# Two transformer layers on one core: where the causal mask of 384- and 512-key diagonal blocks is added in the row maximum of layer 0

## The chip, the core and the metric

The kernel runs on one core of a Trainium2 chip. Five engines work side by side, each through its own queue in order: TensorE (PE in the profile, PEld for its weight loads), VectorE (DVE), ScalarE (ACT), GpSimd (POOL), and SyncE (SP), which here issues DMAs only. They tell each other of finished work through semaphores. The metric is the device time of one execution in microseconds (us); a kernel's time is the median of its runs.

## The reference, cut to what matters

Two transformer layers act on x of shape 2 x 1024 x 256. Each adds an attention and a feed-forward branch to x. The change touches the attention of layer 0 only: 32 query heads of 8 numbers, 8 key heads (four query heads share one), 1024 positions, with a causal mask:

```python
xn = _layernorm(x)
q = (xn @ Wq + bq)...; k = (xn @ Wk + bk)...; v = (xn @ Wv + bv)...   # 32, 8, 8 heads of 8
q = q * cos + rotate_half(q) * sin;  k = k * cos + rotate_half(k) * sin
scores = einsum('bhqd,bhkd->bhqk', q, k_rep) / sqrt(8)
scores = where(kpos > qpos, -inf, scores)
attn = softmax(scores);  out = einsum('bhqk,bhkd->bhqd', attn, v_rep)
x = x + out @ Wo + bo + ffn0(xn)
```

The softmax subtracts each row's maximum over the keys up to the row's own position. Layer 1 has another attention without a causal mask and its own feed-forward branch; it follows after layer 0.

## The kernel before, in words

Layer 0 takes queries in 16 tiles of 128 rows, written (b, i): batch b is 0 or 1, i from 0 to 7. The order is (0,0) to (0,7), then (1,7) down to (1,0). Each tile is handled twice.

**First pass, the maximum** (`max_unit`). For one head pair (16 pairs `p`; the two heads of a pair lie in the upper and the lower 64 rows of the TensorE array, index `e`), TensorE multiplies queries by keys (line 1012) into two PSUM tiles of 512 columns, one for each e, and VectorE takes the negated maximum of each with one `tensor_reduce` from PSUM (line 1024) into a column of the tile `mx`. Tiles with i > 3 first have 16 units over 512 keys that need no mask (`part` 1). Then come the units of the diagonal block (`part` 0, `masked`). Their width is 128, 256, 384 or 512 keys for i mod 4 = 0, 1, 2 or 3, and a unit holds n = 4, 2, 1 or 1 head pairs. The mask is added by TensorE: `add_mask` (line 984) multiplies an identity matrix (`ident_h`) by a triangle of -1e30 (`mask_q`) into the last 128 columns, with four products and four weight loads for one head pair (two halves t, two heads e), 128 and 64 columns wide. The maximum can start when the last of them is done.

**Second pass, the weights** (`weigh`, `gather`). TensorE forms the scores again, transposed and with the maximum folded in as additional rows (line 1076); ScalarE takes the exponential (line 1086); GpSimd zeroes what is above the diagonal (line 1090); TensorE multiplies by the values (line 1106).

PSUM tiles of the first pass come from the pool `ps_s` with three buffers (tag "s"). A unit needs two, so the second product of a unit waits until a maximum of the unit ahead has been read; TensorE's order is written out by hand (`manual_schedule`), so all that stands behind that product waits too. The function `one_slot` sets that order: a credit in columns (`cost`) decides how many units of the first pass go ahead of each piece of the second pass, and pieces of layer 0's feed-forward branch (`ffn0`, lines 216 to 318 on VectorE) and other preparations are dealt out between them. The order of the other engines comes from a scheduler, in queues that run strictly in order.

Constants (`ident_h`, `mask_q`, both made by GpSimd at the start) lie in the pool `zp`, which is freed after layer 0; scratch tiles of layer 0's attention come from `pool`.

Of the kernel before, what the change touches and what calls it, by code (L numbers as in the profile page):

```python
# [10 lines left out]
F32 = mybir.dt.float32  # L11
BF = mybir.dt.bfloat16
# [4 lines left out]
ALU = mybir.AluOpType  # L17
# [3 lines left out]
P = 128  # L21
# [16 lines left out]
NEG = -1e30  # L38
# [11 lines left out]
def two_layers(ctx: ExitStack, tc: tile.TileContext, a: dict, out: bass.AP):  # L50
    nc = tc.nc
    cp = ctx.enter_context(tc.tile_pool(name="const", bufs=1))
    layer0 = ExitStack()
    zp = layer0.enter_context(tc.tile_pool(name="layer0", bufs=1))
# [20 lines left out]
    for name, op, fill, sign in (  # L75
# [5 lines left out]
        for e in range(2):  # L81
            for t in range(2):
                part = m[HALF * e : HALF * e + HALF, t, :]
                nc.gpsimd.affine_select(
                    out=part,
                    in_=part,
                    compare_op=op,
                    fill=fill,
                    base=sign * HALF * t,
                    pattern=[[-sign, P]],  # L90
                    channel_multiplier=sign,
                )
    ident_h, mask_q = both.values()
    groups = cp.tile([P, P], BF, tag="groups", name="groups")
    nc.vector.memset(groups, 0.0)
    nc.vector.memset(groups[0:64, 0:64], 1.0)
# [695 lines left out]
    def attention0(w, qlast, tables):  # L792
# [10 lines left out]
        scale = 1.0 / HD0**0.5  # L803
        with ExitStack() as es:
            pool = es.enter_context(tc.tile_pool(name="a0", bufs=2))
# [170 lines left out]
            def add_mask(out, start, stop):  # L976


                for t in range(2):
                    lo = HALF * t  # L980
                    for e in range(2):
                        rows = slice(HALF * e, HALF * e + HALF)
                        rhs = mask_q[rows, t, None, lo:]
                        nc.tensor.matmul(  # L984
                            out[e][:, :, lo:],
                            ident_h[rows, t, :],
                            rhs.to_broadcast([HALF, out[e].shape[1], P - lo]),
                            start=start and t == 0,
                            stop=stop and t == 1,
                        )  # L990
# [6 lines left out]
            mx = {}  # L997
            reduced = None

            def max_unit(b, i, pairs, lo, width, part, masked):  # L1000
                if (b, i) not in mx:
                    mx[b, i] = pool.tile([P, 2, 2, NH0 // 2], F32, tag="mx", name=f"mx{b}{i}", bufs=3)
                n = len(pairs)
                assert (b, lo // 512) in loaded
                sc = [ps_s.tile([P, 512], F32, tag="s", name=f"m{b}{i}_{pairs[0]}_{part}{e}") for e in range(2)]
                four = masked and width == P
                if four:
                    add_mask([x.rearrange("p (h k) -> p h k", h=4) for x in sc], True, False)
                for s, p in enumerate(pairs):
                    for e in range(2):  # L1010
                        rows = slice(HALF * e, HALF * e + HALF)
                        nc.tensor.matmul(  # L1012
                            sc[e][:, s * width : (s + 1) * width],
                            qst[b, i][0][rows, p, :],
                            kst[b][0][rows, lo // 512, p // 4, 0:width],
                            start=not four,
                            stop=s == n - 1 if four else not masked,
                        )
                    if masked and not four:
                        end = (s + 1) * width  # L1020
                        add_mask([x[:, None, end - P : end] for x in sc], False, True)
                nonlocal reduced
                for e in range(2):
                    reduced = nc.vector.tensor_reduce(  # L1024
                        mx[b, i][:, part, e, pairs[0] : pairs[0] + n],
                        sc[e][:, : n * width].rearrange("p (s k) -> p s k", s=n),
                        AX.X,
                        ALU.max,
                        negate=True,
                    )  # L1030
# [27 lines left out]
            def max_units(b, i):  # L1058

                if i > 3:  # L1060
                    for p in range(16):
                        yield 1024, lambda p=p: max_unit(b, i, [p], 0, 512, 1, False)
                lo = 512 * (i // 4)
                width = (i % 4 + 1) * P
                n = (4, 2, 1, 1)[i % 4]
                for p in range(0, 16, n):
                    yield 2 * n * width, lambda p=p: max_unit(b, i, list(range(p, p + n)), lo, width, 0, True)
                yield 0, lambda: take_max(b, i)
# [375 lines left out]
```

## Time and profile before

| | |
|---|---|
| median of three runs | 1149.86 us (1149.62 to 1157.1) |
| profiled execution, own time | 1152.2 us |
| its span, first to last instruction | 1150.4 us |
| mean granted TensorE clock | 0.927 |
| PE / DVE / ACT / POOL busy, share of the span | 88% / 66% / 53% / 35% |
| line 1024, maxima on VectorE | 608 instructions, 373.0 us busy |
| line 984, mask products on TensorE | 832 products, 73.7 us busy |

Busy time of TensorE overlaps with itself, since products are pipelined and the two halves of the array run side by side: 73.7 us of mask products are not 73.7 us of time. What a line is worth is told by the chain of waits, which follows the work that ended last back from the end. All of the first pass lies between 45 us and 734 us of the span; layer 1 fills the rest.

### The profile page before, as it was taken

What the parts mean: (1) busy time and instruction counts of PE and PEld (TensorE: products, weight loads), DVE (VectorE), ACT (ScalarE), POOL (GpSimd) and SP (SyncE); (2) the same over time, 40 slices, a digit from 0 to 9 for tenths busy, and PEclk for the clock granted to TensorE, in tenths of its full rate; (3) what the DMA queues carried; (4) which work ended last, traced back from release to release, by engine and by line L of the source; (5) the groups of instructions that cost most, each with busy time, mean ns of one, the idle gap of its engine ahead of it and who ended that gap; (6) DMA issues with size and microseconds to landing.
All of it is one profiled execution on the core that took longest, in us unless ns stands there. A gap on an engine that the chain in (4) does not pass through costs nothing.

```text
span 1150.4 us, 19967 instructions
## 1 busy us (share of the span) xinstructions
PE 1008.0 (88%) x7676; PEld 483.0 (42%) x7699; DVE 761.3 (66%) x1434; ACT 607.9 (53%) x1097; POOL 400.4 (35%) x440
## 2 busy tenths in 40 slices
PE   5858797897998989998989989987999999898897
PEld 2333332232432313232323333334567677576576
DVE  6567977889687898889796879413554544543531
ACT  3014571674455757688867766852564444433431
POOL 2007224324135121412123254554744535413400
PEclk9758896998899989999999999998899999989998
DMA  5432101101102010100010110008522332331100
GB/s 176 120 103 75 53 2 40 21 21 41 55 3 51 6 28 10 37 10 8 21 24 5 28 26 6 5 7 103 86 49 47 79 58 43 82 63 34 39 20 20
DMA packets 65927, 49.04 MB, mean 43 GB/s; under 512 B 20904, under 2 KB 59432, under 8 KB 65832
## 3 DMA queue, kind: packets, MB, share of 16 engines
q1 hardware_dynamic: 60632, 39.05, 15.0%
q0 software_dynamic: 4112, 8.26, 3.0%
q8 instruction: 60, 0.98, 0.4%
q10 hardware_dynamic: 1088, 0.46, 0.1%
q14 instruction: 35, 0.29, 0.1%
HBM read 34.12 MB, written 15.20 MB: 43 GB/s over the span
## 4 chain that ended last, share of the span: by engine, by line
PE 53%; DVE 25%; DMA 8%; ACT 6%; POOL 3%; issue 3%; SPq 2%; DVEq 0%; ACTq 0%; POOLq 0%
DVE mx L1024 13%; PE acc L1106 8%; PE s L1076 7%; PE f1gu L672 5%; PE sk L551 4%; PE f1o L711 3%; PE m L1012 3%; PE pqk L465 3%; PE sq L516 3%; DMA qscr<-ptq 2%; PE gu L301 2%; ACT p L1086 2%; DMA qs<-mscr 2%; SPq L936 2%; DMA qkv<-all 2%
## 5 line engine op out<-in xcount | busy, mean ns | idle before, releaser
L1024 DVE TENSOR_REDUCE mx<-m 128x1 f32<-128x512 f32 (+3 forms) x608 | 373.0, 653 | 99.8 <-PE m L1012 53.3
L1086 ACT ACTIVATE p<-s 128x512 f32<-128x512 f32 x576 | 307.6, 606 | 123.1 <-PE s L1076 119.1
L1106 PE MATMUL acc<-p,v 128*9 128x512 f32 x1152 | 170.4, 610 | 1.8 <-ACT p L1086 1.2
L1090 POOL TENSOR_SCALAR_AFFINE_SELECT p<-p 128x512 f32<-128x512 f32 x128 | 83.0, 673 | 152.6 <-ACT p L1086 152.4
L1012 PE MATMUL m<-k,qmain 64*128 64x512 bf16 (+3 forms) x384 | 95.1, 357 | 43.7 <-DVE mx L1024 34.4
L1012 PE MATMUL m<-kmain,qmain 64*128 64x512 bf16 (+3 forms) x384 | 81.7, 330 | 21.8 <-DVE mx L1024 19.9
L1012 PEld LDWEIGHTS <-qmain 64*128 64x128 bf16 x768 | 50.3, 98 | 80.9 <-issue 52.0
L984 PEld LDWEIGHTS <-ident_h 64*128 64x128 bf16 x832 | 45.7, 97 | 82.7 <-issue 59.8
L984 PE MATMUL m<-mask_q,ident_h 64*128 64x128 bf16 (+3 forms) x832 | 73.7, 221 | 1.8 <-DVE mx L1024 1.7
L1076 PE MATMUL s<-qmain,k 64*128 64x512 bf16 x288 | 65.7, 394 | 6.3 <-DVE att L1129 2.7
L1076 PE MATMUL s<-qmain,kmain 64*128 64x512 bf16 x288 | 65.3, 385 | 6.7 <-ACT p L1086 4.2
L1076 PE MATMUL s<-qlast,k 35*128 35x512 bf16 x288 | 62.8, 390 | 0.0
L1076 PE MATMUL s<-qlast,klast 35*128 35x512 bf16 x288 | 61.5, 381 | 0.0
L1076 PEld LDWEIGHTS <-k 64*128 64x128 bf16 (+1 forms) x576 | 21.0, 95 | 93.0 <-issue 84.5
L672 PEld LDWEIGHTS <-wgu_bf 128*128 128x128 bf16 x384 | 38.5, 101 | 42.4 <-issue 6.8
L681 DVE SCALAR_TENSOR_TENSOR h<-h,f1gu 128x512 f32<-128x512 f32 x32 | 22.0, 686 | 51.6 <-ACT h L680 51.6
L686 POOL TENSOR_TENSOR sq<-h 128x512 f32<-128x512 f32 x28 | 29.1, 1040 | 70.3 <-DVE h L682 67.5
L551 PE MATMUL sk<-qs,ks 25*128 25x128 f32 x512 | 45.3, 424 | 7.7 <-DMA qs<-mscr 7.6
L1149 POOL TENSOR_TENSOR x<-x,aos 128x256 f32<-128x256 f32 x16 | 12.6, 788 | 112.6 <-ACT aos L1148 112.6
L559 ACT ACTIVATE p<-sk 128x2048 f32<-128x2048 f32 x16 | 30.0, 1878 | 41.0 <-PE sk L551 41.0
L524 DVE TENSOR_REDUCE m<-sq 128x16 f32<-128x2048 f32 x16 | 36.6, 2287 | 21.8 <-PE sq L516 21.7
L154 POOL TENSOR_TENSOR hp<-hrest,hp 128x512 bf16<-128x512 f32 x32 | 37.0, 1157 | 34.8 <-ACT hp L153 34.8
(288 smaller groups left out, 1803.1 us busy)
## 6 DMA issues: line engine op xcount, KB each, us to landing
qmain<-qscr SPq DMA_DIRECT2D x64, 96.0 KB
qkv<-all SPq DMA_DIRECT2D x16, 384.0 KB
qscr<-ptq POOLq DMA_DIRECT2D x6, 384.0 KB, 4.2
x<-in_x SPq DMA_DIRECT2D x16, 128.0 KB
qmain<-qscr SPq DMA_DIRECT2D x32, 64.0 KB
qs<-qkv SPq DMA_DIRECT2D x16, 128.0 KB
ks<-qkv SPq DMA_DIRECT2D x16, 128.0 KB
vs<-qkv SPq DMA_DIRECT2D x16, 128.0 KB
```

What stands on the lines that cost most here:

```text
L154: engines[1].tensor_tensor(parts[2], r, parts[1], ALU.subtract)
L465: nc.tensor.matmul(pqk, x[k], wqk[:, k, :], start=(k == 0), stop=(k == 1))
L524: last(nc.vector.tensor_reduce(m, ps, AX.X, ALU.max, negate=True))
L551: nc.tensor.matmul(ps[:, s, r, :], columns(k, slice(S * s, S * s + HD + 9), 4 * b + r), columns(q, slice(S * s, S * s + HD + 9), 4 * b + r ...
L672: nc.tensor.matmul(ps[g], wgu_bf[:, k, g * HID + hc * P : g * HID + (hc + 1) * P], x_parts[n][m][:, k, :], start=(k == 0 and m == 0), stop ...
L984: nc.tensor.matmul(out[e][:, :, lo:], ident_h[rows, t, :], rhs.to_broadcast([HALF, out[e].shape[1], P - lo]), start=start and t == 0, stop ...
L1012: nc.tensor.matmul(sc[e][:, s * width : (s + 1) * width], qst[b, i][0][rows, p, :], kst[b][0][rows, lo // 512, p // 4, 0:width], start=not ...
L1024: reduced = nc.vector.tensor_reduce(mx[b, i][:, part, e, pairs[0] : pairs[0] + n], sc[e][:, : n * width].rearrange("p (s k) -> p s k", s=n ...
L1076: nc.tensor.matmul(sc[e], kst[b][n][rows, j // 4, u, j % 4 * P : (j % 4 + 1) * P], qst[b, i][n][rows, 4 * u : 4 * u + 4, :], start=n == 0, ...
L1086: nc.scalar.activation(p, sc[e], AF.Exp, scale=scale)
L1090: nc.gpsimd.affine_select(out=by_head, in_=by_head, compare_op=ALU.is_ge, fill=0.0, base=0, pattern=[[0, 4], [1, P]], channel_multiplier=-1,)
L1106: nc.tensor.matmul(acc[32 * s : 32 * s + HD0 + 1, :], vst[b][:, j, 4 * G + s, :], ps[s], start=(j == 0), stop=(j == i),)
```

## The change

For units of one head pair (n = 1, that is i mod 4 = 2 with 384 keys and i mod 4 = 3 with 512 keys) the four mask products are left out. VectorE takes the maximum with `tensor_tensor_reduce` in the place of `tensor_reduce`: it adds the scores in PSUM to a tile of float32 in SBUF (`later_keys`, -1e30 after the diagonal and 0 elsewhere, its last 384 or 512 columns), multiplies by -1 and takes the minimum into the column of `mx`. The instruction also writes its elementwise result, to a bfloat16 tile `unused` with one buffer that nobody reads. Units with n = 4 and n = 2 keep their mask products, and units without a mask keep `tensor_reduce`. GpSimd makes `later_keys` at the start with two instructions. The area of SBUF that holds descriptors of DMAs issued by GpSimd is set to 4096 bytes of a partition.

```diff
     ident_h, mask_q = both.values()
+    later_keys = zp.tile([P, 512], F32, tag="later_keys", name="later_keys")
+    nc.gpsimd.memset(later_keys, 0.0)
+    nc.gpsimd.affine_select(out=later_keys, in_=later_keys, compare_op=ALU.is_ge, fill=NEG,
+        base=512 - P, pattern=[[-1, 512]], channel_multiplier=1)
...
-                            stop=s == n - 1 if four else not masked,
-                        )
-                    if masked and not four:
+                            stop=s == n - 1 if four else not masked or n == 1,
+                        )
+                    if masked and not four and n > 1:
                         end = (s + 1) * width
                         add_mask([x[:, None, end - P : end] for x in sc], False, True)
                 for e in range(2):
+                    if masked and n == 1:
+                        unused = pool.tile([P, 512], BF, tag="unused", name=f"unused{b}{i}{pairs[0]}{e}", bufs=1)
+                        reduced = nc.vector.tensor_tensor_reduce(
+                            out=unused[:, 0:width],
+                            in0=sc[e][:, 0:width],
+                            in1=later_keys[:, 512 - width : 512],
+                            scale=-1.0,
+                            scalar=-NEG,
+                            op0=ALU.add,
+                            op1=ALU.min,
+                            accum_out=mx[b, i][:, part, e, pairs[0] : pairs[0] + 1],
+                        )
+                        continue
                     reduced = nc.vector.tensor_reduce(
...
-    nc = _bacc.Bacc("TRN2", target_bir_lowering=False, num_devices=1)
+    nc = _bacc.Bacc("TRN2", target_bir_lowering=False, num_devices=1, dynamic_dma_scratch_size=4096)
```

## The prediction, made before the changed kernel was run

> **What bounds the kernel now.** I read the chain of waits first, then the groups by line with shapes kept apart, then the timeline inside one masked tile. The chain on the profile's page says that layer 0 alternates between two engines: VectorE's maxima are the largest line, TensorE's products share the rest.
>
> ```profile
> PE 53%; DVE 25%; DMA 8%; ACT 6%; POOL 3%; issue 3%; SPq 2%; DVEq 0%; ACTq 0%; POOLq 0%
> DVE mx L1024 13%; PE acc L1106 8%; PE s L1076 7%; PE f1gu L672 5%; PE sk L551 4%; PE f1o L711 3%; PE m L1012 3%; PE pqk L465 3%; PE sq L516 3%; DMA qscr<-ptq 2%; PE gu L301 2%; ACT p L1086 2%; DMA qs<-mscr 2%; SPq L936 2%; DMA qkv<-all 2%
> ```
>
> The groups by line give the prices of what is replaced and of what goes. The reader is to see that a maximum over 512 columns takes 681 ns and that the mask products are many and short.
>
> ```profile
> L1024 DVE TENSOR_REDUCE mx<-m 128x1 f32<-128x512 f32 x384 | 245.2, 681 | 54.3 <-PE m L1012 35.0 <-PE m L984 18.8
> L1024 DVE TENSOR_REDUCE mx<-m 128x1 f32<-128x384 f32 x128 | 66.0, 548 | 11.9 <-PE m L984 11.5
> L984 PE MATMUL m<-mask_q,ident_h 64*128 64x128 bf16 x384 | 57.3, 227 | 0.0
> L984 PE MATMUL m<-mask_q,ident_h 64*128 64x64 bf16 x384 | 52.0, 197 | 0.0
> ```
>
> The timeline inside tile (0,7), whose 32 maxima of 512 masked keys are replaced, shows the ping-pong: two units give VectorE four maxima in a row, then it waits 1.52 us for the next mask product, while TensorE's second unit (line 1012, 0.88 us instead of 0.38) waits for the first maximum to free its buffer.
>
> ```profile
> 383.83 0.24 PE L984 MATMUL m<-mask_q,ident_h 64*128 64x128 bf16 x4
> ...
> 384.11 2.51 DVE L1024 TENSOR_REDUCE mx<-m 128x1 f32<-128x512 f32 x4 [1.52 <-PE m L984]
> 384.13 0.38 PE L1076 MATMUL s<-qlast,k 35*128 35x512 bf16 x2
> 384.13 0.10 PEld L1012 LDWEIGHTS <-qmain 64*128 64x128 bf16 x2
> 384.35 0.88 PE L1012 MATMUL m<-k,qmain 64*128 64x512 bf16 x2
> ...
> 384.86 0.45 PE L984 MATMUL m<-mask_q,ident_h 64*128 64x128 bf16 x4
> ```
>
> The replaced maxima lie in eight stretches, found by following the reductions tile by tile: 78.0 to 123.0, 123.3 to 160.6, 309.7 to 333.6, 373.0 to 404.3, 435.8 to 468.9, 500.0 to 525.7, 630.5 to 665.0 and 666.6 to 697.6, together 261.8 us. The windows view gives VectorE 218.7 us of busy time in them, 84%. Of its 43 us of idle time 31 lie directly before a replaced maximum, in front of 50 of the 256. The chain of waits, taken in these stretches, holds 68 us of line 1024 and 10 us of line 984.
>
> **What goes.** 8 tiles of 16 units lose four products and four weight loads: 512 of the 832 of line 984. On the chain that is 10 us, not 512 x 0.2, because the two halves of the array run together and the products overlap with their neighbours. In tile (0,7) the chain from one pair of units to the next reads: maximum 0.69, m 0.23, mask 0.22, gu 0.97, acc 0.97, s 0.54, m 0.22, mask 0.13, sum 3.97 us; the masks are 0.35 of it.
>
> **What comes: one instruction becomes two.** In the order of the built program VectorE has 1685 rows in place of 1429, 256 more. Each replaced maximum is the elementwise instruction and a second one that writes the single column of `mx`; the semaphore that frees the PSUM buffer is raised by the second alone. And because `unused` has one buffer, each waits for the second instruction of the one before it, by a separate wait on VectorE's own semaphore, ahead of the wait for TensorE. In 146 of the 256 cases nothing stands between the two in VectorE's queue, in 110 something does.
>
> Prices, each from a row. (a) The main instruction: lines 681 and 682 also take 512 float32 from PSUM and as many from SBUF and write 512; they take 687 ns, against 681 now, so +0.01. (b) The own wait: line 682 waits in just this form, for VectorE's previous instruction and then for a product that is long done. It starts 0.80 after line 681 did. The four maxima above, which depend on nothing of VectorE's, take 2.51 us, so they start (2.51 - 0.68) / 3 = 0.61 apart. The own wait costs 0.19, the overlap of 0.08 and a gap of 0.11.
>
> ```profile
> 869.39 0.69 DVE L681 SCALAR_TENSOR_TENSOR h<-h,f1gu 128x512 f32<-128x512 f32 x1 [1.52 <-ACT h L680]
> 870.19 0.69 DVE L682 SCALAR_TENSOR_TENSOR h<-h,f1gu 128x512 f32<-128x512 f32 x1
> ```
>
> (c) The second instruction: no row shows one. It is no gain, since it can't end before the first. Its nearest rows from below and above are a memset of 128x1, 59 ns, and line 185, 128x2, 165 ns, of which 0.08 overlaps; even without overlap and with a gap of its own it is 0.2. I take 0.08 and keep 0.0 and 0.2.
>
> ```profile
> L99 DVE MEMSET ones<- x1: 59/59/59, 1.0 to 1.0; 128x1 f32 x1
> ```
>
> So an adjacent replaced maximum costs 0.27 us more of VectorE's time, any other 0.08: 146 x 0.27 + 110 x 0.08 = 48 us. Where VectorE was idle before the maximum the own wait is hidden by that idleness: up to 50 x 0.19 = 10 us off, 39 to 48 us.
>
> The Trainium skill bears on (b): "VectorE: DVE Perf Modes", section "The DRAIN you can't avoid", says that a semaphore after each of a row of copies cost nothing. This trace has 0.80 against 0.61 and decides; by the page 146 x 0.19 = 28 us would go from the sum and the change would come out near no change or faster. It also bears on (a): "Vector Engine (DVE) Microarchitecture Reference", section "Points that are easy to get wrong", says that this family of instructions runs at half speed with two sources in SBUF that aren't bfloat16. Here one source is in PSUM, as in line 681, which runs at full speed; by the page, and as an estimate from the 128 x 0.61 + 128 x 0.48 us that they take now, half speed would cost some 140 us more.
>
> **The sum.** Two ways bound it. Old chain, new prices: of the 256, 122 are on the chain, 67 of them adjacent: 67 x 0.27 + 55 x 0.08 = 22, less about 5 for own waits under idleness, less 10 of masks: +8 us. That is a floor if the prices hold, since a chain under new prices can only be overtaken by a longer one. VectorE's work: 218.7 + 48 = 267 us must pass in the eight stretches, and about 14 us of idleness in the first two waits for DMAs (rope 8.2, query tiles 5.8 on the chain) that nothing shortens: 281, so +19; if a third of the 31 us of idleness before maxima stays because arrivals are uneven, +30. I take **+18**: 1152.2 + 18 = 1170 for a profiled execution. The profiled one before lay 2.3 us above its median, so the median should be **1168 us**.
>
> **Costed at nothing.** GpSimd's two new instructions (a memset as 128x576 at 0.58, a selection like line 1090's at 0.67) put off the first weight load from 5.3 to about 6.6 us; VectorE uses it at 29.3. Without that cover: 1.2 us. The smaller descriptor area: GpSimd issues at most six loads in a row; were it to wait for one to land, that is up to 8.6 us, in a stretch where GpSimd then sits idle for 23 us. ScalarE and GpSimd have the same instructions, a few moved by one or two places. The bfloat16 result is written while the instruction reads.
>
> **The rivals.**
> - *TensorE's path decides, faster.* If the second instruction and own wait fit into VectorE's idle time, only the first maximum of each four stays on the chain: 0.69 + 0.08, and 0.35 less masks, 3.70 in place of 3.97 for two units. 64 such pairs give -17; by the chain's own 10 us, -10. So 1133 to 1140. For it: the 1.52 us of idleness in tile (0,7). Against it: there four maxima grow from 2.5 to 3.5 us of 3.7, and VectorE has some 80 us of other work in the eight stretches (218.7 less 128 x 0.61 and 128 x 0.48, the latter from 548 ns and the overlap). It turns where an adjacent maximum costs under about 0.1 us more. Chance 0.13.
> - *A wash, within 1%.* Gains and losses cancel at a second instruction near 0 us; 1142 to 1159. Chance 0.25.
> - *The new instruction is slow.* Line 151, 128x512 of float32 with two operands, averages 982 ns beside GpSimd where line 864 takes 691. At +0.3 for all 256 it is 77 us more: 1245. For it: an operand in SBUF while GpSimd works there. Against it: lines 681 and 682, never over 690 ns with GpSimd half busy. Chance 0.07.
> - *It doesn't do what it says.* The built program lacks the 512 products, so only prices are open.
>
> **The numbers.** A 1% change, 11.5 us, is about what a measurement of this kernel can tell from none. My forecast (slower, 1160 to 1205) has 0.55; its upper end is the second instruction at 0.2 us, which adds 256 x 0.12 = 31 us to +18. With the slow instruction, slower by over 1% has 0.62, within 1% 0.25, faster 0.13. The range leaves out the slow instruction and most of the faster case: 1144 to 1205.
>
> **What would show it.** Right: about 320 rows of line 984; the replaced maxima near 0.69 us and their seconds under 0.2; VectorE over 95% busy in the eight stretches; adjacent main instructions near 0.87 apart; TensorE waiting more on `mx`. Wrong: idleness of VectorE before maxima as long as now with the second instruction short (then faster), or a main instruction well over 0.7 (then far slower).

## The result and the profile after

The changed kernel took **1179.65 us**, the median of 4 runs (1177.52 to 1182.22), beside 1151.43 us for the kernel before on the same chip (its three runs and a fourth): a ratio of 1.0237 with a 95% interval of 1.0211 to 1.0262, so 28 us slower. The profiled execution took 1177.52 us, its span 1175.6 us at a mean granted clock of 0.916 (before: 1152.2, 1150.4 and 0.927).

Lines of the kernel after have other numbers: the products (before L1012) are L1023 and the mask products (L984) L995, higher by 11; the maxima of unmasked and narrower units (L1024) are L1048, higher by 24; the replaced maxima are L1037. The chain of waits on the page of the kernel after, by engine and by line:

```profile
PE 51%; DVE 26%; ACT 6%; DMA 6%; issue 5%; POOL 4%; SPq 1%; DVEq 0%; ACTq 0%; POOLq 0%
PE acc L1130 8%; DVE mx L1048 8%; PE s L1100 7%; DVE unused L1037 7%; PE f1gu L683 5%; PE m L1023 4%; PE f1o L722 3%; PE sk L562 3%; PE pqk L476 3%; PE sq L527 2%; PE gu L312 2%; ACT p L1110 2%; DMA qs<-mscr 1%; DMA qkv<-all 1%; PE ot L1145 1%
```

The maxima are still its largest part: L1048 and L1037 hold 15% of a longer span, where L1024 held 13%. The mask products are not among the lines listed, neither before nor after; 320 of the 832 are left (L995, 28.9 us busy). The groups by line with shapes kept apart (line, engine, operation, count, busy us, mean ns of one, idle time before them and what ended it):

```profile
L1048 DVE TENSOR_REDUCE mx<-m 128x1 f32<-128x512 f32 x256 | 163.1, 680 | 36.7 <-PE m L1023 36.3
L1037 DVE CUSTOM_DVE_ANT_0 unused<-m,later_keys 128x512 bf16<-128x512 f32 x128 | 87.9, 686 | 22.7 <-PE m L1023 12.8 <-PE s L1100 0.2
L1037 DVE CUSTOM_DVE_ANT_0 unused<-m,later_keys 128x384 bf16<-128x384 f32 x128 | 70.7, 553 | 26.0 <-PE m L1023 13.9 <-PE s L1100 2.1 <-DVE mx L1037 0.5
L1037 DVE DVE_READ_ACCUMULATOR2_ANT mx<- 128x1 f32 x256 | 21.0, 82 | 0.0
```

The replaced maximum is as quick as the plain one: 686 against 681 ns for 512 columns, 553 against 548 for 384. Its second instruction reads the accumulator in 82 ns. The Trainium skill says as much of the form, without a price ("VectorE: DVE Perf Modes", section "Two Vector instructions with no wait between them": an operation that also writes out its accumulator is two instructions). What is new is the idleness that nothing in this answer explains: of the 48.7 us before L1037 only 29.5 are put down to another engine or to `mx`.

The timeline of VectorE in tile (0,7) shows where the rest lies (start us, duration us, engine, line, operation):

```profile
391.72 0.69 DVE L1037 CUSTOM_DVE_ANT_0 unused<-m,later_keys 128x512 bf16<-128x512 f32 x1
392.33 0.08 DVE L1037 DVE_READ_ACCUMULATOR2_ANT mx<- 128x1 f32 x1
392.56 0.69 DVE L1037 CUSTOM_DVE_ANT_0 unused<-m,later_keys 128x512 bf16<-128x512 f32 x1
393.18 0.08 DVE L1037 DVE_READ_ACCUMULATOR2_ANT mx<- 128x1 f32 x1
393.18 0.42 DVE L227 TENSOR_SCALAR fe<-fw 128x1024 uint16<-128x1024 uint16 x1
```

The read starts 0.61 after the main instruction, while that still runs for 0.07 to 0.08. An instruction that doesn't wait for the read (L227) starts together with it. An adjacent replaced maximum does wait for it: it starts 0.23 after the read did, 0.84 after the maximum ahead of it. Over all 146 adjacent cases the gap between a read's end and the next start is 144 ns in the median; in 131 of them it lies between 100 and 200 ns.

The windows view, by the eight stretches of the replaced maxima in each kernel (length, then busy time and number of PE, PEld, DVE, ACT and POOL, granted clock, DMA share, GB/s); here the kernel after, tiles (0,2) and (0,6), and the sum over eight:

```profile
77.60:130.80 53.20, 39.93 (x146) 13.46 (x149) 32.23 (x93) 15.89 (x28) 23.26 (x25) 0.79 0.31 88
...
321.30:349.70 28.40, 25.12 (x158) 7.08 (x150) 23.47 (x80) 16.50 (x33) 5.23 (x8) 0.88 0.05 20
...
sum 288.70, PE 244.17 PEld 69.16 DVE 230.04 ACT 177.56 POOL 72.34; mean PE 30.52 PEld 8.64 DVE 28.76 ACT 22.20 POOL 9.04
```

The stretches are 288.7 us long instead of 261.8, so 26.9 us are lost in them, and the whole span is 25.2 us longer. VectorE is busy for 230.0 us instead of 218.7: its idle time in them grew from 43 to 59 us, although it has more to do. Some 21 us of that (146 x 0.144) are the gaps between adjacent maxima.

### The profile page after: what moved, and what is told of

Read it like the earlier page. It is cut to its first block, busy times and chain, and to the rows that moved or that the text cites. A ratio compares the mean times of both kernels' runs of the same rounds, so it can differ in the third digit from the quotient of the medians.

```text
span 1175.6 us, 19438 instructions
## 1 busy us (share of the span) xinstructions
PE 1016.5 (86%) x7187; PEld 459.9 (39%) x7187; DVE 775.1 (66%) x1690; ACT 609.1 (52%) x1097; POOL 397.6 (34%) x442
## 4 chain that ended last, share of the span: by engine, by line
PE 51%; DVE 26%; ACT 6%; DMA 6%; issue 5%; POOL 4%; SPq 1%; DVEq 0%; ACTq 0%; POOLq 0%
PE acc L1130 8%; DVE mx L1048 8%; PE s L1100 7%; DVE unused L1037 7%; PE f1gu L683 5%; PE m L1023 4%; PE f1o L722 3%; PE sk L562 3%; PE pqk L476 3%; PE sq L527 2%; PE gu L312 2%; ACT p L1110 2%; DMA qs<-mscr 1%; DMA qkv<-all 1%; PE ot L1145 1%
## 5 line engine op out<-in xcount | busy, mean ns | idle before, releaser
L1048 DVE TENSOR_REDUCE mx<-m 128x1 f32<-128x512 f32 (+2 forms) x352 | 225.0, 681 | 69.3 <-PE m L1023 54.6
L1037 DVE CUSTOM_DVE_ANT_0 unused<-m,later_keys 128x384 bf16<-128x384 f32 (+1 forms) x256 | 158.6, 620 | 48.7 <-PE m L1023 26.7
L1130 PE MATMUL acc<-p,v 128*9 128x512 f32 x1152 | 175.1, 628 | 4.6 <-POOL p L1114 3.0
L1023 PE MATMUL m<-k,qmain 64*128 64x512 bf16 (+3 forms) x384 | 95.8, 359 | 49.8 <-DVE mx L1048 28.7
L1023 PE MATMUL m<-kmain,qmain 64*128 64x512 bf16 (+3 forms) x384 | 85.0, 337 | 28.1 <-DVE mx L1037 14.1
L1023 PEld LDWEIGHTS <-qmain 64*128 64x128 bf16 x768 | 51.5, 99 | 100.2 <-issue 75.7
L1100 PE MATMUL s<-qmain,kmain 64*128 64x512 bf16 x288 | 68.6, 398 | 7.8 <-ACT p L1110 4.0
L1100 PE MATMUL s<-qmain,k 64*128 64x512 bf16 x288 | 68.3, 405 | 7.5 <-DVE att L1153 3.2
L1100 PE MATMUL s<-qlast,klast 35*128 35x512 bf16 x288 | 64.4, 394 | 0.0
L1130 PEld LDWEIGHTS acc<-p,v 128*9 128x9 f32 x1152 | 19.9, 89 | 85.7 <-issue 60.5
```

The source lines that it names most:

```text
L1023: nc.tensor.matmul(sc[e][:, s * width : (s + 1) * width], qst[b, i][0][rows, p, :], kst[b][0][rows, lo // 512, p // 4, 0:width], start=not ...
L1037: reduced = nc.vector.tensor_tensor_reduce(out=unused[:, 0:width], in0=sc[e][:, 0:width], in1=later_keys[:, 512 - width : 512], scale=-1.0 ...
L1048: reduced = nc.vector.tensor_reduce(mx[b, i][:, part, e, pairs[0] : pairs[0] + n], sc[e][:, : n * width].rearrange("p (s k) -> p s k", s=n ...
L1100: nc.tensor.matmul(sc[e], kst[b][n][rows, j // 4, u, j % 4 * P : (j % 4 + 1) * P], qst[b, i][n][rows, 4 * u : 4 * u + 4, :], start=n == 0, ...
L1130: nc.tensor.matmul(acc[32 * s : 32 * s + HD0 + 1, :], vst[b][:, j, 4 * G + s, :], ps[s], start=(j == 0), stop=(j == i),)
```

## The experiments

In the expectations, Theory 1 puts the loss down to the own wait of adjacent maxima; the others put it elsewhere in the change or in its setup, as each text says. The following table puts all kernels side by side; "six later" is the summed length of tiles (0,6), (0,7), (1,7), (1,6), (1,3) and (1,2), "first two" that of (0,2) and (0,3), both from the profiled execution by the windows view. "Setup" is `later_keys` made at the start and the descriptor area of 4096 bytes. The last column compares each kernel with the one before on the same chip, with a 95% interval.

| kernel | mask products | replaced maxima | setup | first two | six later | median us | ratio to before |
|---|---|---|---|---|---|---|---|
| before | all | none | none | 82.3 | 179.5 | 1151.4 to 1152.8 | |
| after | out | 1 buffer | both | 91.7 | 197.0 | 1179.65 | 1.0237 [1.0211, 1.0262] |
| bufs2 | out | 2 buffers | both | 87.9 | 178.0 | 1157.29 | 1.0052 [1.0028, 1.0075] |
| bufs4 | out | 4 buffers | both | 87.4 | 178.1 | 1156.89 | 1.0048 [1.0025, 1.0070] |
| both_masks | all | 1 buffer | both | 87.9 | 195.8 | 1175.12 | 1.0204 [1.0163, 1.0245] |
| no_mask | out | none | both | 87.0 | 176.1 | 1159.97 | 1.0073 [1.0048, 1.0098] |
| setup_only | all | none | both | 83.5 | 178.6 | 1159.05 | 1.0055 [1.0029, 1.0082] |
| bufs4_masks | all | 4 buffers | both | 82.1 | 181.2 | 1158.18 | 1.0037 [1.0015, 1.0058] |
| late_only | out in six | 4 buffers, in six | both | 82.4 | 178.3 | 1156.79 | 1.0035 [1.0014, 1.0056] |
| no_mask_late | out in six | none | both | 83.3 | 176.3 | 1156.73 | 1.0035 [1.0013, 1.0057] |
| scratch_only | all | none | area | 82.9 | 178.7 | 1156.64 | 1.0025 [1.0007, 1.0044] |
| keys_only | all | none | keys | 80.6 | 178.6 | 1153.96 | 1.0006 [0.9983, 1.0029] |
| keys_later | out | 4 buffers | keys, behind the loads | 89.5 | 177.9 | 1154.14 | 1.0009 [0.9990, 1.0028] |
| masks_out | out | none | none | 88.7 | 176.4 | 1156.43 | 1.0031 [1.0013, 1.0050] |

### The own wait

**bufs4.** Only the number of buffers of `unused` differs from the kernel after, so that a replaced maximum need not wait for the one before it.

```diff
-                        unused = pool.tile([P, 512], BF, tag="unused", name=f"unused{b}{i}{pairs[0]}{e}", bufs=1)
+                        unused = pool.tile([P, 512], BF, tag="unused", name=f"unused{b}{i}{pairs[0]}{e}", bufs=4)
```

> The changed kernel with four buffers of unused in place of one, so that 253 of the 256 replaced maxima wait for TensorE alone and no longer for VectorE's own instruction before. Theory 1 (the own wait is the loss): in the changed kernel an adjacent maximum starts 843 ns after the one before, 227 of them after the column read has started; without the wait that becomes about 0.62, VectorE's extra time falls from 37 to about 4 us and the 10 to 17 us of masks come out: 1134 to 1142 us. Theory 2 (two instructions and the later release of the PSUM buffer are the loss, the wait lies in time when VectorE would be idle anyway): 1165 to 1180 us.

It took 1156.89 us, which lies in neither range: what Theory 1 says of the wait is what the timeline shows, but the gain from the masks that it counted on is missing. The timeline of VectorE in tile (0,7) of this kernel:

```profile
381.78 0.68 DVE L1037 CUSTOM_DVE_ANT_0 unused<-m,later_keys 128x512 bf16<-128x512 f32 x1
382.39 0.08 DVE L1037 DVE_READ_ACCUMULATOR2_ANT mx<- 128x1 f32 x1
382.39 0.69 DVE L1037 CUSTOM_DVE_ANT_0 unused<-m,later_keys 128x512 bf16<-128x512 f32 x1
```

The second maximum now starts with the read of the first, 0.61 after the first instead of 0.84: the pair costs what two plain maxima did. Over all adjacent cases the medians are 0.61 for 512 columns and 0.48 for 384, against 0.84 and 0.71 in the kernel after. The six later tiles fell from 197.0 to 178.1 us, and the eight stretches together by 23 us. By the ratios the own wait is worth 1.0237 - 1.0048, some 22 us of the 28. The scheduler also moved about a dozen instructions of VectorE when the wait went, so the 22 us hold these moves too; no run has the one without the other. The granted clock of TensorE rose too in those tiles (0.88 to 1.00 in (0,6)). That it is no cause of its own is seen in both_masks, below, where (0,6) has the waits and a clock of 1.00 and still takes 27.4 us, against 28.4 after and 23.2 here.

**bufs2.** The same line with `bufs=2`: a maximum waits for the one before last.

> Two buffers of unused: 147 replaced maxima still have a separate wait on VectorE's own semaphore, but for the maximum before the last, which is done by then. Theory 1 (the time until the own instruction is done is the loss): within 3 us of four buffers. If the separate wait instruction itself costs, whatever it waits for, about 100 ns for each of 147: 10 to 15 us above four buffers. Theory 2: 1165 to 1180 us, as with four.

It took 1157.29 us, level with four buffers, as Theory 1 had it, and VectorE's order is the same as with four. The source view of the line in this kernel has 147 separate waits of 21 ns on VectorE's queue, where bufs4 has 3:

```profile
L1037 DVEq EVENT_SEMAPHORE  x147: 21/21/21, 103.3 to 699.2; - x147
```

So a separate wait costs nothing that can be measured here (adjacent maxima start 0.61 apart, as with four); a wait for the read directly ahead does: the next maximum then starts 144 ns after the read has ended, where without the wait it starts together with the read.

### What the mask products were worth

**both_masks.** The kernel after with the mask products of before kept as well (the mask is added twice).

```diff
-                            stop=s == n - 1 if four else not masked or n == 1,
+                            stop=s == n - 1 if four else not masked,
...
-                    if masked and not four and n > 1:
+                    if masked and not four:
```

> The changed kernel with the mask products of 384 and 512 keys kept as well; the mask is then added twice. It has all that the change adds and none of what it takes away. Theory 1: the old chain's 10 us of masks come back only in part, because VectorE is the limit in these tiles: 1182 to 1192 us. Were TensorE's path the limit, all of 0.17 us for each of 128 units: over 1195 us.

It took 1175.12 us, below the 1182 to 1192 that were expected and not more than the kernel after. Keeping 512 products that nobody needs cost nothing that can be measured.

**no_mask.** The kernel after with the plain maximum in the place of the new one: neither way of masking, everything else of the change (`if masked and n == 1:` becomes `if False:`).

> The kernel before without the mask products of 384 and 512 keys and with the maximum as before, so that these maxima are taken over the later keys too (the mask is left out of them). It has what the change takes away and nothing that it adds on VectorE. By the old chain 10 us less than before, by the two-unit period 17 less: 1134 to 1142 us. If the products were hidden: 1150 us. Four buffers should lie within 4 us above it.

It took 1159.97 us, far from the 1134 to 1142 that were expected and 8 us above before, though it only leaves work out and adds the setup. With bufs4, which is no slower, this says that the replaced maxima themselves, once they needn't wait for one another, cost nothing that can be told from the rest.

**masks_out.** Free of the setup: the kernel before, without the mask products of these units.

```diff
-                            stop=s == n - 1 if four else not masked,
+                            stop=s == n - 1 if four else not masked or n == 1,
...
-                    if masked and not four:
+                    if masked and not four and n > 1:
```

> The kernel before without the 512 mask products of the units of one head pair, and nothing else changed: no later_keys, no smaller descriptor area, the plain maxima of before. The mask of those units is left out of the maximum, so this computes another thing; it is run for its time alone. It isolates the prediction's term of 10 us for masks on the chain, free of the setup that all earlier kernels without masks carried. If that term is right and was covered up by the setup: 1138 to 1144 beside a before of 1152. If the products around the masks and the maxima take up the time (the six later tiles of earlier kernels without masks were 0.3 to 0.9 us shorter each): 1146 to 1151. If tile (0,2) also becomes longer by some 5 us without its masks, as in the earlier kernels that left them out there (49.7 and 50.6 against 45.0), even without the setup: 1150 to 1156.

It took 1156.43 us, 1.0013 to 1.0050 times before, just above the third of the expected ranges: leaving out 512 products and as many weight loads made the kernel slower by 4 us. The table says where: the six later tiles are 3.1 us shorter, the first two 6.4 longer. (Of the 3.1 us, 0.9 may be chance: setup_only, scratch_only and keys_only have the code of before in these six tiles and take 178.6 to 178.7 us, not 179.5, since (1,2) runs at a granted clock of 1.00 in them and of 0.94 in the trace of before.) Two views show more.

The chain of waits of masks_out in tile (0,7), for one pair of units (start us, us, what):

```profile
389.36 0.69 DVE mx L1024
390.06 0.04 issue
390.10 0.37 PE m L1012
390.47 0.97 PE gu L301 x4
391.44 0.98 PE acc L1106 x8
392.42 0.54 PE s L1076 x4
392.95 0.26 PE m L1012 x2
393.22 0.69 DVE mx L1024
```

From maximum to maximum it is 3.86 us. Before, from 384.12 to 388.15, it was 4.03, with mask products of 0.22 and 0.13 in it; the parts of that chain that differ:

```profile
384.86 0.23 PE m L1012
385.09 0.22 PE m L984 x3
...
387.80 0.22 PE m L1012 x2
388.02 0.13 PE m L984 x4
```

Those 0.35 are gone, but only 0.17 are gained: the product of the second unit takes 0.37 of the chain where it took 0.23, and that of the first 0.26 where it took 0.22. The likely reason, which no run tests by itself, is that the mask products ran beside the end of the product ahead of them, and that without them what follows waits for that end. Of eight pairs at 0.17, 1.4 us, the tile keeps 0.4.

In tile (0,2) the next query tiles are projected in float32 (L849), three sets of eight products whose duration follows the granted clock: most take 592 ns (as in 94.05 to 97.70 of before, where the clock is 1.00) or 1061 ns (as in 95.84 to 98.50 of masks_out, where it is 0.50). Windows of (0,2) and the three sets on TensorE's timeline, before:

```profile
78.00:123.00 45.00, 36.44 (x205) 15.93 (x205) 31.40 (x60) 15.85 (x28) 25.53 (x25) 0.88 0.37 100
```

```profile
78.08 5.39 PE L849 MATMUL q010p<-xnT,wq 128*128 128x512 f32 x8
87.74 5.40 PE L849 MATMUL q011p<-xnT,wq 128*128 128x512 f32 x8 [0.26 <-DVE q010y L860]
94.05 3.70 PE L849 MATMUL k01p<-xnT,wk 128*128 128x512 f32 x8
```

and masks_out:

```profile
78.50:129.70 51.20, 39.99 (x146) 13.79 (x149) 30.20 (x62) 15.84 (x28) 24.77 (x25) 0.78 0.31 91
```

```profile
78.73 6.35 PE L849 MATMUL q010p<-xnT,wq 128*128 128x512 f32 x8 [0.22 <-DVE mx L1024]
85.01 0.33 PE L1012 MATMUL m<-k,qmain 64*128 64x384 bf16 x1
85.99 0.32 PE L1012 MATMUL m<-k,qmain 64*128 64x384 bf16 x1 [0.65 <-DVE mx L1024]
86.96 1.98 PE L849 MATMUL q011p<-xnT,wq 128*128 128x512 f32 x4 [0.65 <-DVE mx L1024]
89.22 1.98 PE L849 MATMUL q011p<-xnT,wq 128*128 128x512 f32 x4 [0.27 <-DVE q010y L860]
...
93.95 0.32 PE L1012 MATMUL m<-k,qmain 64*128 64x384 bf16 x1 [2.05 <-DVE q011y L860]
95.84 6.35 PE L849 MATMUL k01p<-xnT,wk 128*128 128x512 f32 x8 [1.56 <-DVE q011y L860]
```

The order on VectorE changed as well. Its timeline in masks_out around the first step behind the projection:

```profile
85.38 0.56 DVE L1024 TENSOR_REDUCE mx<-m 128x1 f32<-128x384 f32 x1 [5.24 <-PE m L1012]
86.35 0.56 DVE L1024 TENSOR_REDUCE mx<-m 128x1 f32<-128x384 f32 x1 [0.41 <-PE m L1012]
86.82 1.22 DVE L224 TENSOR_TENSOR wg<-fsw,few 128x1024 bf16<-128x1024 f32 x1
88.07 0.43 DVE L226 TENSOR_SCALAR wg<-wg 128x1024 bf16<-128x1024 bf16 x1
88.42 1.40 DVE L860 SCALAR_TENSOR_TENSOR q010y<-q010p,bq,rope 128x512 f32<-128x512 f32 x2
```

Before, VectorE took `q010y` first, and the maxima and `wg` after it:

```profile
86.28 1.41 DVE L860 SCALAR_TENSOR_TENSOR q010y<-q010p,bq,rope 128x512 f32<-128x512 f32 x2 [6.61 <-DMA rope<-in_rope]
87.60 1.01 DVE L1024 TENSOR_REDUCE mx<-m 128x1 f32<-128x384 f32 x2
88.53 1.65 DVE L224 TENSOR_TENSOR wg<-fsw,few 128x1024 bf16<-128x1024 f32 x1
```

In masks_out the scheduler put those first, and `q010y` starts at 88.42. TensorE then stands idle from 91.9 to 95.8 but for one product, and the last set of projections, behind which the rest of the tile stands in TensorE's queue, runs at the lower clock: 6.35 instead of 3.70 us, ending at 102.2 instead of 97.7, which is 3.9 us later counted from the start of the tile. The other 2.3 us arise behind it. The kernels after, bufs4 and keys_later have the same picture (the last set takes 6.25, 6.32 and 6.37 us).

The low clock is the smaller part of the loss. bufs2 has the same order of `q010y` behind the maxima and `wg` and the same two waits of 2.05 and 1.56 us, but its last set takes 5.40 us and its clock in the tile is 0.86:

```profile
79.10:129.30 50.20, 37.26 (x145) 12.52 (x149) 31.72 (x94) 15.89 (x28) 24.20 (x25) 0.86 0.32 91
```

At that clock it still takes 50.2 us, while before, scratch_only and setup_only, which keep the mask products, take 45.0 to 46.5 at 0.87 or 0.88. So some 4 to 5 us go with the missing mask products and the order that comes with them; which of the moved steps costs them is not shown. Nor is it shown that the idleness brings the low clock: no run changed the one without the other.

### The setup

**setup_only.** The kernel before with all of the setup and none of the rest.

```diff
+    later_keys = zp.tile([P, 512], F32, tag="later_keys", name="later_keys")
+    nc.gpsimd.memset(later_keys, 0.0)
+    nc.gpsimd.affine_select(...)
...
-    nc = _bacc.Bacc("TRN2", target_bir_lowering=False, num_devices=1)
+    nc = _bacc.Bacc("TRN2", target_bir_lowering=False, num_devices=1, dynamic_dma_scratch_size=4096)
```

> The kernel before with later_keys made at the start (and not used) and the smaller descriptor area; mask products and maxima as before. The kernel without mask products was 8 us slower than before, most of it lost in the first masked tile (0,2), where float32 projections ran at half the TensorE clock. Theory A (missing mask products and shifted maxima there let TensorE idle, and the clock with it): 1150 to 1154 us, as before. Theory B (the setup, 1.1 us of GpSimd ahead of the first weight load or the smaller descriptor area, shifts that tile): 1157 to 1160 us.

It took 1159.05 us, 1.0029 to 1.0082 times before, in Theory B's range. GpSimd's timeline at the start shows the two instructions, and the first weight load issued at 6.38 instead of 5.34:

```profile
2.97 0.53 POOL L95 MEMSET later_keys<- 128x512 f32 x1
...
4.78 0.61 POOL L96 TENSOR_SCALAR_AFFINE_SELECT later_keys<-later_keys 128x512 f32<-128x512 f32 x1
5.34 1.09 POOL L954 MEMSET v<- 128x576 f32 x2
6.38 1.28 POOL L251 DMA_DIRECT2D spare_main<-in_w_gating  x2
```

The orders on VectorE and ScalarE are those of before. Tile (0,2) starts 3.7 us later (81.7 instead of 78.0), and the masked units of (0,4) 6.8 us later (210.5 instead of 203.7); the last tile, (1,0), is 6.9 us late (726.2 instead of 719.4). So in this trace all of the loss arises in the first 210 us, where the work waits for loads and projections, and the tiles behind keep their lengths to about a microsecond. The loads themselves land a little later: the view of the DMAs gives 7.9 and 9.4 us from issue to landing for the first two pairs, instead of 6.9 and 8.6.

**scratch_only** and **keys_only** each take one half of it: the first sets the descriptor area to 4096 bytes and makes no `later_keys`, the second makes `later_keys` with an area of 15360 bytes (there is no room for both `later_keys` and the 16384 of before).

> The kernel before with one edit: the descriptor area is set to 4096 bytes of a partition; later_keys isn't made and the maxima are those of before. The kernel before with the whole setup of the change but none of its maxima took 1159.05, 7 us more than before. Theory K, the 1.1 us of GpSimd's two instructions ahead of the first weight load are what costs: 1150 to 1154, as before. Theory S, the smaller area (or the addresses that move with it) costs: 1157 to 1160. Theory V, any shift of the early chain of latencies costs a few us, whichever edit makes it: 1153 to 1160.

> The kernel before with the other edit of the setup: GpSimd makes later_keys at the start (a memset and a selection, 1.1 us, ahead of the first weight load); nothing reads it. The descriptor area is 15360 bytes, the nearest to before's 16384 that leaves room for later_keys. Theory K: 1157 to 1160. Theory S: 1150 to 1154. Theory V: 1153 to 1160.

scratch_only took 1156.64 us (1.0007 to 1.0044), keys_only 1153.96 (0.9983 to 1.0029). A cost of GpSimd's 1 us by itself is thus not to be told from none, and Theory K falls as the whole cause; the smaller area, or the addresses that move with it, carries perhaps half of the 6 us. Of the three theories only V, whose ranges are the widest, holds both times. Why the two together cost more than their sum stays open: the three intervals overlap, and the twelve times of keys_only lie anywhere from 1149.0 to 1162.0, wider than what is to be explained.

**keys_later.** bufs4, with `later_keys` made by GpSimd behind the first weight loads, and an area of 11264 bytes.

```diff
+            with tc.issue_after(last_load[0].ins):
+                later_keys = zp.tile([P, 512], F32, tag="later_keys", name="later_keys")
+                nc.gpsimd.memset(later_keys, 0.0)
+                nc.gpsimd.affine_select(...)
```

> The changed kernel with four buffers for the unused result, and with GpSimd making later_keys behind the first weight loads instead of ahead of them; descriptor area of 11264 bytes. With later_keys ahead of the loads and 4096 bytes, four buffers gave 1156.89 against 1151.9 before. Theory K: the 5 us of the start come back, 1146 to 1152, level with before or a little faster. Theory S: back only if 11264 bytes are enough, 1146 to 1157, together with scratch_only at 1157 or more. Theory V: another order at the start gives another few us, in either direction, 1148 to 1160.

It took 1154.14 us, 0.9990 to 1.0028 times before, above Theory K's range and within V's. This is the quickest form of the change among these runs, and no different from before.

### Mixed forms

**bufs4_masks**: bufs4 with the mask products of before kept as well. **late_only**: bufs4 in the six later tiles, the way of before in (0,2) and (0,3). **no_mask_late**: late_only with the plain maximum, so that the six later tiles are not masked in it.

```diff
-                    if masked and n == 1:
+                    if masked and n == 1 and (b == 1 or i > 5):
```

> Four buffers of unused, and the mask products of 384 and 512 keys kept (the mask is added twice). Against four buffers alone it tells what the mask products are worth on the new VectorE path, against the kernel before what the two-instruction maximum is worth. Theory A: the tile (0,2) is as in the kernel before, and the maximum costs 15 ns each where VectorE is the limit: 1152 to 1156 us, no slower than four buffers alone. Theory B: 1158 to 1165 us.

> The change with four buffers, in the six later tiles alone ((0,6), (0,7) and those of batch 1); (0,2) and (0,3) keep their mask products and plain maxima. Theory A: the early loss does not arise and the six tiles gain 0.3 to 0.9 us each: 1146 to 1151 us. Theory B: 1154 to 1158 us.

> Plain maxima everywhere, the mask products left out in the six later tiles (their maxima run over later keys too), kept in (0,2) and (0,3). Theory A: 1146 to 1150 us, within 2 us of the change in the six tiles. Theory B: 1154 to 1158 us.

They took 1158.18, 1156.79 and 1156.73 us, in the ranges of Theory B each time, and their ratios lie within the intervals of bufs4 and setup_only. Their worth is in the table's two columns of lengths: with four buffers the first two tiles are 82.1 and 82.4 us long where their mask products stay, 87.4 where they go. In the six later tiles four buffers give 181.2 with the products and 178.1 without. So leaving the products out pays 2 to 3 us in the later tiles and costs 5 in tile (0,2); against the plain maxima with their masks (178.6 to 179.5 us) the change with four buffers gains only 0.5 to 1.4 us in the later tiles. In the medians these gains and losses don't add up to more than the setup's few us and its spread.

## Why the prediction was right, and where its sum was not

**The direction and its cause** held. The forecast was slower, 1168 us within 1144 to 1205; the time was 1179.65. The own wait of adjacent maxima was priced as the main cost, and bufs4 shows it to be some 22 of the 28 us. That the number came out within 12 us is in part luck, as the sum below shows.

**(a) The main instruction**, +0.01 us: 686 and 553 ns against 681 and 548. The half speed that the prediction weighed doesn't come, as the row of line 681 had said.

**(b) The own wait**, 0.19 us: 0.23 (0.84 against 0.61). The Trainium skill's statement that a semaphore after each of eight copies cost nothing extra ("VectorE: DVE Perf Modes", section "The DRAIN you can't avoid") doesn't carry over to this case: with the wait for the instruction directly ahead the kernel takes 1179.65 us, without it 1156.89. In bufs2, where the wait is for an instruction that has long ended, it costs nothing here either.

**(c) The second instruction**, 0.08 us within 0 to 0.2: it takes 82 ns, but starts 74 ns before the main one ends, so that a next instruction that doesn't wait for it comes 0.61 after the first, as with plain maxima. It adds about 0.01. The sum on VectorE was therefore 146 x 0.24 + 110 x 0.01, some 36 us, not 48.

**Less 10 us of masks** is the term that was furthest off. It stands in the floor of +8 and in the price of the faster rival, not in the +18 that was taken. The 10 us were read off the chain of waits, as if what follows would move up by all that a link is long. In a pair of tile (0,7) only 0.17 of 0.35 us is gained, since the products around the masks take more of the chain; the six later tiles gain 2 to 3 us, tile (0,2) loses more than that in another order, and masks_out is 4 us slower.

**Costed at nothing**: keys_only shows no cost of GpSimd's two instructions that can be told from none (0.9983 to 1.0029), as their cover (a load that is used only at 29.3 us) had it. Yet the whole setup makes the kernel before 6 us longer (1.0029 to 1.0082). The case kept for the smaller area, a load that waits for another to land, isn't what the profile shows: its loads are issued one behind the other as before.

**The sum**: +18 was taken, between +8 by the old chain and +19 or +30 by VectorE's work, and +28 came. It goes by VectorE's work: 267 us of it and 14 of idleness were to fill the eight stretches, 281 in all. They took 288.7. VectorE's work, gaps included, grew to 251 us only (230.0 + 21), and 38 us of idleness remained, more than the 14 to 25 that were allowed. So 16 us too much of work stand against some 24 too little of idleness, and the two partly cancel: the direction was argued from the right cost, but that the sum came as near as it did is luck.

**The rivals.** The faster one was to decide where an adjacent maximum costs under 0.1 us more. bufs4 and keys_later meet that condition (0.61 apart) and give 1157 and 1154, not 1133 to 1140, since the gain from the masks isn't there and the setup costs a few us. They are what the wash describes. The slow instruction didn't come (686 ns), and the 512 products are gone.

**What would show it**: about 320 rows of mask products (320), 0.69 us and under 0.2 for the two instructions, 0.87 between adjacent ones (0.84) and more waiting of TensorE for maxima (54.3 us of idleness ahead of the two groups of L1012 before, 69.9 ahead of those of L1023 after) were right. VectorE over 95% busy was wrong: 80%, or 87% with the gaps.

## What to carry to other kernels

An output that nobody reads still needs buffers: with one, every instruction here waited for the end of the one before it, on its own engine, and on a path of short alternating steps that was worth 22 us. Price an operation taken from the chain not by its length there but by what the chain will hold in its place: of 0.35 us of mask products half came back as longer products around them. Where a scheduler orders the queues, look also at what moves beside the edit: without its mask products tile (0,2) had another order on VectorE and was 4 to 6 us longer, more than the six later tiles gained.

## What was not expected of the hardware

The read of an accumulator (82 ns) overlaps with its main instruction by 74 ns, and the next instruction can start together with it, unless it waits for it: then a gap of 144 ns follows (medians of the kernel after). A separate wait of 21 ns for something that has ended costs no time (147 of them in bufs2). A float32 product of 128x512 takes 592 ns at a granted clock of 1.00 and 1061 at 0.50, so that a set of eight moved by 2.6 us (3.70 and 6.35). And one program's times lie over more than 10 us in its runs (keys_only, 1149.0 to 1162.0), so that a few us between two single traces say nothing; the lengths of the later tiles repeat better, to 0.1 us in the sum of six among setup_only, scratch_only and keys_only, and to 0.9 with before.
